# Macaron block (FFN, Mamba scan, FFN) on one core: down products issued in three parts, the next stage's transposes behind the second part

## The chip, the cores and the metric

The kernel runs on one core of a Trainium2 chip. The metric is the device time of one execution in microseconds (us). Before the change the median of three executions is 3233.29 us (3232.2 to 3233.48). A further execution, taken by the profiler, is the source of every row that is shown below.

## What is computed

The input has B, L, H = 4, 1024, 512: 4096 rows of 512 numbers, all fp32. The reference, cut to what matters:

```python
x = x + 0.5 * ffn(layernorm(x))           # stage 1
x = x + mamba(layernorm(x))
x = x + 0.5 * ffn(layernorm(x))           # stage 2

def ffn(x):                               # INTER = 1408
    g = (x @ gate_w.T) * gate_s
    u = (x @ up_w.T) * up_s
    return ((silu(g) * u) @ down_w.T) * down_s

def mamba(x):                             # I = 1024, N = 16, K = 4, R = 128
    h, gate = split(W_in @ x)
    h = silu(causal_conv(h, conv_w) + conv_b)
    ts, Bm, Cm = split(Wx @ h)            # R, N and N numbers, each RMS-normalised
    delta = softplus(Wdt @ ts + dt_bias)
    for t in range(L):                    # in each batch
        s = exp(delta[t] * A) * s + delta[t] * Bm[t] * h[t]
        y[t] = sum_n(s * Cm[t])
    return (Wout @ ((y + D * h) * silu(gate)))
```

## The kernel before

**Chunks and tiles.** The rows are scanned in 16 chunks (`NCS`) of 256 rows, one after another, numbered 0 to 15. The two FFN stages work on tiles of 128 rows. They are not passes of their own: while chunk k is scanned, the FFN of three or four tiles is computed beside it, some of stage 1 for chunks to come, some of stage 2 for chunks already done. The list `BESIDE` fixes how many of each: 3, 3, 4, 4, 3, 4, 4, 3, 4, 4, 3, 4, 4, 3, 3, 3 for chunks 0 to 15. "A three-tile chunk" below means a chunk with three tiles beside it. An FFN has `NF` = 11 blocks of 128 hidden columns; so the down product of one tile is 11 matmuls, each 128x128 by 128x512, summed in one PSUM tile.

**The scan.** In a chunk there are 8 groups of channels (index i) and 4 groups of states (index g), 32 units. In a unit (`unit`) each half does this: ACT makes two exponentials (`da`, L573), POOL a product (`sb`, L578), DVE two scans (L582), a copy of the last state (L587) and a multiplication (`sb`, L592). A half is called a pair in the prediction, since its two scans, its copy and its multiplication go together. Later `add_up` sums a unit's `sb` into `yps` on TensorE, by four matmuls of 128x32 by 128x256 (L604); the sums of an i go out four units at a time. When an i is complete, DVE adds D times u (L611). `head` prepares the step sizes of two further i: the product `dp` of TensorE (L490), which reads `tsT`, then `z` and `dd` on ACT (L498 to L503) and corrections on POOL (L506 to L521). The rest of the preparation is by chunk: the products `hp` for the convolution (L376) and `gp` for the gate (L545), the parameters, and their transposes with the copy into `tsT` (L455).

**The background list.** What lies beside the scan of chunk k is a list of `Work` parts made by `background(k)`. A part has a cost (columns of TensorE work), a share of DVE work (`vector`), a function that emits its instructions, and possibly weight blocks to be loaded. The main loop emits a unit of the scan, then takes parts from the list as long as the part of TensorE's cost done so far is behind the part of DVE's work done so far. A part is never cut: all its instructions come out in one go.

The order in the list is: loads, the first products of the next chunk's preparation, the FFN's `gate_w` and `up_w` products (both L273), between them the gate projections, the output product `op` of the chunk before (L635) and the convolution. The end of the list is what the change touches. There stand the down products (`fo`, L319) and the transposes of the next chunk's FFN tiles (`tp`, L235, made by `flips`). `flips` gives one part that starts the statistics of the first two tiles, and then one part for each tile. That part does a tile's four transposes, defers the copy out of PSUM (L238), and starts the statistics of the tile two further on: `stf` and `mvf` on DVE (L209, L210), `vef`, `rsf`, `nbf` on POOL (L214 to L216), and the normalised tile `xnf` on ACT (L218).

Before, the list ends thus, where `turn` is what `flips` gave and `weave` puts the second list's entries behind the first's:

```python
w, turn = weave(turn[1:2] + f.down(), [NOTHING] + turn[2:])
return parts + w + turn
```

So the order is: transposes of next tile 0, product 0 (all 11 matmuls), transposes of next tile 1, product 1, transposes of next tile 2, and so on.

**What else orders the work.** `defer` holds an emission back until so many further parts with a cost are out; the addition of a down product to its tile (L327) is deferred by one such part, and the store of the tile is handed to SP when two further parts of any kind are out. All loads and stores go through SP's queue, in program order (L101). Weights go through a ring of 14 slots, filled up to 12 blocks ahead. PSUM has a pool of three tiles ("mm") for all products but `da` and `yps`. Instructions that are "pinned" keep their program order on their engine; the others may be moved by the framework's scheduler when the program is built. On the chip each engine runs its list in order.

Of the kernel before, what the change touches and what calls it, by code (L numbers as in the profile page):

```python
# [8 lines left out]
F32 = mybir.dt.float32  # L9
# [4 lines left out]
P = 128  # L14
B, L, H = 4, 1024, 512
# [6 lines left out]
NF = INTER // P  # L22
# [11 lines left out]
HALVES = 14  # L34
LEAD = 12
FRONT = 5
RING = 14

BESIDE = [(3, 0), (3, 0), (2, 2), (2, 2), (1, 2), (2, 2), (2, 2), (2, 1), (2, 2), (2, 2), (2, 1), (2, 2), (2, 2), (1, 2), (0, 3), (0, 3)]
# [3 lines left out]
def macaron_kernel(ctx: ExitStack, tc: tile.TileContext, a: dict, out: bass.AP):  # L43
# [8 lines left out]
    p8 = ctx.enter_context(tc.tile_pool(name="p8", bufs=8))  # L52
    ring = ctx.enter_context(tc.tile_pool(name="ring", bufs=RING))
    dram = ctx.enter_context(tc.tile_pool(name="scratch", bufs=1, space=bass.MemoryType.DRAM))
# [3 lines left out]
    ps_m = ctx.enter_context(tc.tile_pool(name="ps_m", bufs=3, space=PSUM))  # L58
# [27 lines left out]
    down_w = [dram.tile([P, H], F32, name=f"down_w{it}") for it in range(NF)]  # L86
# [56 lines left out]
    def store(out, in_):  # L143
        stores.append([0, out, in_])
# [9 lines left out]
    def defer(parts, emit):  # L154

        deferred.append([parts, emit])
# [7 lines left out]
    def settle():  # L164
        while deferred:
            deferred.pop(0)[1]()
# [18 lines left out]
    NOTHING = Work(0, 0, lambda: None)  # L185

    def then(f, *args):
        return Work(0, 0, lambda: f(*args))

    def cols(t):  # L190
        return t.rearrange("p (k o) -> p k o", k=KH)
# [5 lines left out]
    def silu(t):  # L197

        pin(nc.scalar.activation(t, t, AF.Silu))
        pin(nc.scalar.preload_act_table_set("natural_log_exp_and_others"))  # L200
# [42 lines left out]
    class FFN:  # L243
# [35 lines left out]
        def gate(self):  # L279
            self.done = 0  # L280

            def part(it):
                def emit(w):
                    if it == 0:
                        self.hd = p1.tile([P, NF, 2 * T], F32, tag="hd", name=f"hd{self.name}")
                    gp = self.product("gate_w", it, w[0])
                    nc.scalar.activation(  # L287
                        self.hd[:, it, : self.n], gp, AF.Copy, scale=gate_s[:, it : it + 1]
                    )
                    if it % 4 == 3 or it == NF - 1:  # L290
                        h = self.hd[:, self.done : it + 1, : self.n]
                        silu(h)
                        self.done = it + 1

                return Work(KH * self.n, 0, emit, [("gate_w", it)], settled=it == 0)

            return [part(it) for it in range(NF)]
# [10 lines left out]
            return [part(it) for it in range(NF)]  # L308

        def down(self):  # L310
            wd = []

            def part(t):
                def emit(w=None):
                    wd.extend(w or [])
                    nm = f"{self.name}_{t}"
                    op = ps_m.tile([P, H], F32, tag="mm", name=f"fo{nm}")
                    for it in range(NF):
                        nc.tensor.matmul(  # L319
                            op, lhsT=self.hd[:, it, t * P : (t + 1) * P], rhs=wd[it],  # L320
                            start=(it == 0), stop=(it == NF - 1),
                        )
                    x = self.x[t]
                    stage, r = self.tiles[t]

                    def added():
                        pin(nc.vector.tensor_tensor(x, x, op, ALU.add))  # L327
                        store(x1[r] if stage == 1 else out[r * P : (r + 1) * P, :], x)

                    defer(1, added)  # L330

                return Work(NF * H, H, emit, [("down_w", it) for it in range(NF)] if t == 0 else ())

            r = [part(t) for t in range(len(self.tiles))]
            r[0].until, r[0].settled = r[-1], True
            return r

# [29 lines left out]
    def prep_conv(k):  # L367
        def part(i):
            def emit(w):
                if i == 0:  # L370
                    st[k]["u"] = p2.tile([P, NI, T], F32, tag="u", name=f"u{k}")
                u = st[k]["u"]
                hp = ps_m.tile([P, 512], F32, tag="mm", name=f"hp{k}_{i}")
                w = cols(w[0])
                for kk in range(KH):
                    nc.tensor.matmul(  # L376
                        hp[:, : K - 1 + T], lhsT=w[:, kk, :], rhs=st[k]["xnT"][:, kk, :],
                        start=(kk == 0), stop=(kk == KH - 1),
                    )
                nc.scalar.activation(  # L380
                    u[:, i, :], hp[:, 0:T], AF.Identity,
                    bias=conv_b[:, i : i + 1], scale=conv_w[:, i, 0:1],
                )

                def taps():
                    for q in range(1, K):
                        pin(nc.vector.scalar_tensor_tensor(  # L387
                            u[:, i, :], hp[:, q : q + T], conv_w[:, i, q : q + 1], u[:, i, :],
                            ALU.mult, ALU.add,
                        ))  # L390
                    if i == NI - 1:
                        defer(1, lambda: silu(u))

                defer(1, taps)

            return Work(KH * T, 4 * T, emit, [("W_in", i)], settled=i == 0)

        return [part(i) for i in range(NI)]
# [250 lines left out]
    def weave(xs, by):  # L649

        r = []
        for n, w in enumerate(xs):
            r.append(w)
            r += by[n : n + 1]
        return r, by[len(xs) :]
# [32 lines left out]
    first = [(1, r) for r in range(2 * J, NCS * J)]  # L688
# [17 lines left out]
    def background(k):  # L706

        f = ffn[k]
        prep = k + 1 if k + 1 < NCS else None
        gates, out_of = gate(k), tail(k - 1) if k else []  # L710
        turn = flips(None, prep) if prep is not None else []
        conv = params = []
        if prep is not None:
            conv, params = prep_conv(prep), prep_params(prep)
            ready[k] = params[-1]
        parts = [then(tail_load, k - 1)] if k else []
        if prep is not None:
            parts.append(then(prep_load, k + 1))
        parts += turn[:1]
        p = [NOTHING] * (4 if k else 0) + gates + turn[1:] + out_of + conv  # L720
        tiles = (f.gate() if k else []) + f.up()
        p = [p[n : n + 2] for n in range(0, len(p), 2)]
        p += [[NOTHING]] * 4 + [[w] for w in params]
        turn = flips(ffn[k + 1], None) if k + 1 < NCS else []
        for n, w in enumerate(tiles):
            parts.append(w)
            for q in p[n : n + 1]:
                parts += q
            if n == len(tiles) - NF and k + 1 < NCS:
                parts.append(then(ffn[k + 1].load))  # L730
            if n == len(tiles) - NF and k + 1 == NCS:
                parts.append(then(tail_load, k))
                parts.append(then(end_load))
            if n == len(tiles) - 2:
                parts += turn[:1]
        for q in p[len(tiles):]:
            parts += q
        w, turn = weave(turn[1:2] + f.down(), [NOTHING] + turn[2:])
        return parts + w + turn

    ready = {}


    start = FFN("p", [(1, r) for r in range(2 * J)])
    down, gate_0 = start.down(), ffn[0].gate()
    turn_f, turn_m = flips(ffn[0], None), flips(None, 0)
    front = flips(start, None) + start.gate() + [then(load_resident)] + start.up()
    front += [down[0], down[1], then(prep_load, 0), turn_m[0], down[2]] + turn_m[1:]
    front += [turn_f[0]] + weave(prep_conv(0), [down[3]] + turn_f[1:])[0]
    front += weave(gate_0[:FRONT], prep_params(0))[0]  # L750
    beside_scan = [background(k) for k in range(NCS)]
    end = FFN("e", last)
    turn = flips(end, None)
    back_end = tail(NCS - 1) + turn + end.gate() + end.up() + end.down()
    for w in front + gate_0[FRONT:] + [w for b in beside_scan for w in b] + back_end:
        if w.blocks:
# [8 lines left out]
    settle()  # L765
    between = gate_0[FRONT:]
    chores = head(0, 0)
# [16 lines left out]
    for k in range(NCS):  # L784
        more = k + 1 < NCS
        parts, n, done, vector = list(beside_scan[k]), 0, 0, 0
# [121 lines left out]
```

## Time and profile before

| what | value |
|---|---|
| median of three executions | 3233.29 us (3232.2 to 3233.48) |
| the profiled execution | 3235.77 us |
| its span in the profile | 3234.0 us |
| mean granted clock of TensorE | 0.978 |
| `fo` (L319) on TensorE | 547.6 us, 1232 matmuls of 599 ns |
| `gate_w` and `up_w` (L273) | 566.9 and 564.8 us, 1408 matmuls each |
| `yps` (L604) | 318.6 us, 4096 matmuls; idle before them 79.1 us |
| scans (L582) on DVE | 1057.0 us (x1536) and 321.2 us (x512) |
| products `sb` (L578) on POOL | 1275.0 us, 1024 of 1273 ns |
| weights of `down_w`, by SP | 187 loads of 256 KB, median 2.8 us to landing |

The engines' rows of the page give busy time, share of the span and number of instructions. A group's row gives the source line, engine and operation, the tile that is written and what is read, the shapes and the count; behind the bar stand busy time and the mean of one; then the idle time just before them, and what ended most of it. A row of the waits view names the instruction that waited, behind the arrow the one that released it, then the total in us, how often, and the longest. A timeline row has the start and the duration in us, then engine, line, operation and tiles; "x22" says that so many like it are put together in one row, so that the row's duration covers them all and what lay between, and a bracket gives the idle time before it and what ended it.

### The profile page before, as it was taken

The page shows a single profiled execution, that of the slowest core. Times are in us where ns is not written, and L with a number is a line of the kernel's source. Part 1 is how long each engine was busy: PE and PEld are TensorE (multiplying, and loading weights), DVE is VectorE, ACT ScalarE, POOL GpSimd, SP SyncE. Part 2 cuts the span into 40 slices and gives each one's busy share as a digit, 9 for nine tenths or more (in the row PEclk, how much of TensorE's full clock was granted, in tenths as well). Part 3 has the DMA queues.
Part 4 walks back from the last instruction along what each step waited for, and adds up shares of the span by engine and source line. Part 5 has one row for each costly group of instructions (what it writes and reads, how often), then busy time and mean ns, then how long its engine had stood idle before and what let it go on. Part 6 is the DMA issues. An engine that isn't in the chain of part 4 may idle for free.

```text
span 3234.0 us, 41940 instructions
## 1 busy us (share of the span) xinstructions
PE 3057.9 (95%) x12448; PEld 1648.7 (51%) x12448; DVE 2474.3 (77%) x4981; ACT 1787.0 (55%) x3535; POOL 1937.7 (60%) x1895
## 2 busy tenths in 40 slices
PE   8988898999999999999999999989999998989999
PEld 3554454545555454545545555545555554544434
DVE  1259788888869898887979798787969788788831
ACT  3265554747565664747565564747556474655430
POOL 0066857566766757566765757576665756667510
PEclk9999998999999999999999999999999999999999
DMA  5364655646566555547565656655565654546431
GB/s 171 113 175 113 179 163 154 172 126 189 140 180 185 173 167 162 162 130 207 137 176 162 177 163 171 177 138 170 141 183 160 177 167 136 178 114 197 143 96 44
DMA packets 287427, 506.43 MB, mean 157 GB/s; under 512 B 32097, under 2 KB 50273, under 8 KB 287201
## 3 DMA queue, kind: packets, MB, share of 16 engines
q1 hardware_dynamic: 285616, 503.31, 54.8%
q8 instruction: 100, 1.64, 0.2%
q14 instruction: 127, 1.03, 0.1%
q10 hardware_dynamic: 1584, 0.45, 0.1%
HBM read 442.03 MB, written 61.60 MB: 156 GB/s over the span
## 4 chain that ended last, share of the span: by engine, by line
PE 62%; DVE 20%; ACT 8%; POOL 4%; issue 4%; DMA 1%; SPq 0%; DVEq 0%; ACTq 0%; POOLq 0%
PE fo L319 13%; PE gate_w L273 12%; DVE da L582 12%; PE up_w L273 8%; PE yps L604 5%; PE hp L376 5%; PE gp L545 5%; PE op L635 4%; DVE sb L592 4%; ACT da L573 3%; POOL sb L578 2%; PE dp L490 1%; PE gate_wp L273 1%; PE gate_we L273 1%; DVE u L387 1%
## 5 line engine op out<-in xcount | busy, mean ns | idle before, releaser
L578 POOL TENSOR_TENSOR sb<-rep,bc 128x512 f32<-128x512 f32 x1024 | 1275.0, 1273 | 448.7 <-PE yps L604 381.7
L582 DVE TENSOR_TENSOR_SCAN da<-da,state,sb 128x256 f32<-128x256 f32 x1536 | 1057.0, 739 | 287.3 <-ACT da L573 253.1
L573 ACT ACTIVATE da<-rep,a_w 128x256 f32<-128x256 f32 x2048 | 899.3, 470 | 538.1 <-DVE sb L592 523.6
L592 DVE TENSOR_TENSOR sb<-da,bc 128x512 f32<-128x512 f32 x1024 | 687.7, 680 | 0.9
L273 PE MATMUL gate_w<-fxT,w_gate_w 128*128 128x384 f32 (+1 forms) x1408 | 566.9, 549 | 5.6 <-ACT dd L499 2.3
L273 PE MATMUL up_w<-fxT,w_up_w 128*128 128x384 f32 (+1 forms) x1408 | 564.8, 551 | 0.8 <-issue 0.4
L319 PE MATMUL fo<-w_down_w,hd 128*128 128x512 f32 x1232 | 547.6, 599 | 0.0
L273 PEld LDWEIGHTS up_w<-fxT,w_up_w 128*128 128x128 f32 x1408 | 266.9, 194 | 250.0 <-issue 156.7
L273 PEld LDWEIGHTS gate_w<-fxT,w_gate_w 128*128 128x128 f32 x1408 | 267.6, 193 | 247.7 <-issue 152.4
L604 PE MATMUL yps<-sb,fold 128*32 128x256 f32 x4096 | 318.6, 392 | 79.1 <-DVE sb L592 70.9
L582 DVE TENSOR_TENSOR_SCAN da<-da,sb 128x256 f32<-128x256 f32 x512 | 321.2, 680 | 79.2 <-ACT da L573 65.5
L319 PEld LDWEIGHTS fo<-w_down_w,hd 128*128 128x128 f32 x1232 | 231.5, 192 | 274.0 <-issue 265.0
L521 POOL TENSOR_SCALAR e<-z 128x512 f32<-128x512 f32 x64 | 124.2, 1941 | 278.6 <-ACT z L502 241.8
L604 PEld LDWEIGHTS yps<-sb,fold 128*32 128x32 f32 x4096 | 125.7, 110 | 275.4 <-DVE sb L592 128.3
L376 PE MATMUL hp<-mxT,w_W_in 128*128 128x259 f32 x1024 | 242.6, 388 | 24.3 <-issue 12.9
L545 PE MATMUL gp<-mxT,w_W_in 128*128 128x256 f32 x1024 | 241.4, 385 | 4.1 <-ACT dd L499 2.2
L376 PEld LDWEIGHTS hp<-mxT,w_W_in 128*128 128x128 f32 x1024 | 193.2, 192 | 82.4 <-issue 34.1
L635 PE MATMUL op<-w_Wout,u 128*128 128x512 f32 x512 | 225.0, 595 | 4.6 <-issue 3.6
L545 PEld LDWEIGHTS gp<-mxT,w_W_in 128*128 128x128 f32 x1024 | 193.5, 191 | 61.9 <-issue 17.9
L287 ACT ACTIVATE hd<-gate_w,gate_s 128x384 f32<-128x384 f32 (+1 forms) x176 | 110.6, 629 | 167.5 <-PE gate_w L273 166.6
L387 DVE SCALAR_TENSOR_TENSOR u<-hp,conv_w,u 128x256 f32<-128x256 f32 x384 | 177.6, 474 | 17.4 <-ACT u L380 14.7
L304 DVE SCALAR_TENSOR_TENSOR hd<-up_w,up_s,hd 128x384 f32<-128x384 f32 (+1 forms) x176 | 117.7, 669 | 61.5 <-PE up_w L273 61.4
(112 smaller groups left out, 2657.9 us busy)
## 6 DMA issues: line engine op xcount, KB each, us to landing
rep<-row SPq DMA_DIRECT2D x512, 256.0 KB, 5.1
w_W_in<-in_W_in_dram SPq DMA_DIRECT2D x256, 256.0 KB, 3.5
w_gate_w<-in_gate_w_dram SPq DMA_DIRECT2D x198, 256.0 KB, 3.9
w_up_w<-in_up_w_dram SPq DMA_DIRECT2D x198, 256.0 KB, 3.1
w_down_w<-down_w SPq DMA_DIRECT2D x187, 256.0 KB, 2.8
row<-dd SPq DMA_DIRECT2D x128, 256.0 KB, 3.2
w_Wout<-in_Wout_dram SPq DMA_DIRECT2D x128, 256.0 KB, 3.4
bc<-bcd SPq DMA_DIRECT2D x64, 256.0 KB, 4.7
```

Source lines behind the costliest of these rows:

```text
L273: nc.tensor.matmul(o[:, : self.n], lhsT=w[:, k, :], rhs=self.xT[:, k, : self.n], start=(k == 0), stop=(k == KH - 1),)
L319: nc.tensor.matmul(op, lhsT=self.hd[:, it, t * P : (t + 1) * P], rhs=wd[it], start=(it == 0), stop=(it == NF - 1),)
L376: nc.tensor.matmul(hp[:, : K - 1 + T], lhsT=w[:, kk, :], rhs=st[k]["xnT"][:, kk, :], start=(kk == 0), stop=(kk == KH - 1),)
L387: pin(nc.vector.scalar_tensor_tensor(u[:, i, :], hp[:, q : q + T], conv_w[:, i, q : q + 1], u[:, i, :], ALU.mult, ALU.add,))
L521: lambda: pin(nc.gpsimd.tensor_scalar(e, z, 1.0, 1.0, ALU.add, ALU.subtract)),
L545: nc.tensor.matmul(gp[:, :T], lhsT=w[:, kk, :], rhs=st[k]["xnT"][:, kk, K - 1 :], start=(kk == 0), stop=(kk == KH - 1),)
L573: e = nc.scalar.activation(da[:, j, :], rep[:, h + j, 0, :], AF.Exp, scale=a_w[:, b0 + h + j, g : g + 1])
L578: nc.gpsimd.tensor_tensor(sb, rep[:, hs, 1, :], d["bc"][:, g : g + 1, :].to_broadcast([P, 2, T]), ALU.mult)
L582: nc.vector.tensor_tensor_scan(da[:, j, :], da[:, j, :], sb[:, j, :], 0.0 if first else state[:, b0 + h + j, g : g + 1], ALU.mult, ALU.add,)
L592: nc.vector.tensor_tensor(sb, da, d["bc"][:, NS + g : NS + g + 1, :].to_broadcast([P, 2, T]), ALU.mult)
L604: nc.tensor.matmul(yp[j * Q : (j + 1) * Q, :], lhsT=fold, rhs=pr[j // 2][:, j % 2, :], start=(g == 0), stop=(g == NS - 1),)
L635: nc.tensor.matmul(op, lhsT=st[k]["u"][:, i, j * P : (j + 1) * P], rhs=wo[i], start=(i == 0), stop=(i == NI - 1),)
```

## The change

A constant `DOWN` = 4 is added. `FFN.down` gives three parts for each tile in place of one: 4, 4 and 3 of the 11 matmuls. The PSUM tile is taken when the first part is emitted, and the addition to the tile is deferred when the last is. The cost of a part is its own matmuls; the DVE share is counted on the last alone. In `background` the transposes of the next FFN's tiles no longer stand between whole products: the first stand ahead of all of them, and those of tile n + 1 stand behind the second part of product n. In the front, the part ahead of the first scan, each entry of `down` is replaced by its three parts, and the last tile's three parts are woven with the preparation of chunk 0. The number of matmuls, of transposes, of loads and of stores stays.

```diff
+DOWN = 4
         def down(self):
-            wd = []
-
-            def part(t):
+            wd, ops = [], {}
+            bounds = [*range(0, NF, DOWN), NF]
+
+            def part(t, lo, hi):
                 def emit(w=None):
                     wd.extend(w or [])
                     nm = f"{self.name}_{t}"
-                    op = ps_m.tile([P, H], F32, tag="mm", name=f"fo{nm}")
-                    for it in range(NF):
+                    if lo == 0:
+                        ops[t] = ps_m.tile([P, H], F32, tag="mm", name=f"fo{nm}")
+                    op = ops[t]
+                    for it in range(lo, hi):
                         nc.tensor.matmul(
                             op, lhsT=self.hd[:, it, t * P : (t + 1) * P], rhs=wd[it],
                             start=(it == 0), stop=(it == NF - 1),
                         )
+                    if hi < NF:
+                        return
                     x = self.x[t]
...
                     defer(1, added)
 
-                return Work(NF * H, H, emit, [("down_w", it) for it in range(NF)] if t == 0 else ())
-
-            r = [part(t) for t in range(len(self.tiles))]
+                first = t == 0 and lo == 0
+                return Work(
+                    (hi - lo) * H, H if hi == NF else 0, emit,
+                    [("down_w", it) for it in range(NF)] if first else (),
+                )
+
+            r = [part(t, *b) for t in range(len(self.tiles)) for b in zip(bounds, bounds[1:])]
...
-        w, turn = weave(turn[1:2] + f.down(), [NOTHING] + turn[2:])
-        return parts + w + turn
+        parts += turn[1:2]
+        each = -(-NF // DOWN)
+        for n, w in enumerate(f.down()):
+            parts.append(w)
+            if n % each == 1:
+                parts += turn[2 + n // each : 3 + n // each]
+        return parts + turn[2 + len(f.tiles) :]
...
-    front += [down[0], down[1], then(prep_load, 0), turn_m[0], down[2]] + turn_m[1:]
-    front += [turn_f[0]] + weave(prep_conv(0), [down[3]] + turn_f[1:])[0]
+    each = len(down) // len(start.tiles)
+    front += down[: 2 * each] + [then(prep_load, 0), turn_m[0]] + down[2 * each : 3 * each] + turn_m[1:]
+    front += [turn_f[0]] + weave(prep_conv(0), down[3 * each :] + turn_f[1:])[0]
```

## The prediction

> **What bounds the kernel now.** I read the busy shares first, then the windows around one projection stage of each kind, then who waits for whom, then the timeline of the worst stage. Each answer narrows the next question.
>
> ```profile
> PE 3057.9 (95%) x12448; PEld 1648.7 (51%) x12448; DVE 2474.3 (77%) x4981; ACT 1787.0 (55%) x3535; POOL 1937.7 (60%) x1895
> ```
>
> TensorE (PE) is the bound, and the change removes no matmul. Only its idle time (3234.0 - 3057.9 = 176 us), its slow spells and the waits hidden in its busy rows can be won. I took windows of 60 us; columns as in the page's first part, then PEclk, DMA share, GB/s. In order they hold the down products of chunks 1, 2, 4, 10:
>
> ```profile
> 490.00:550.00 60.00, 48.59 (x192) 21.04 (x191) 47.88 (x99) 27.64 (x61) 43.28 (x41) 0.86 0.55 151
> 686.00:746.00 60.00, 60.00 (x229) 29.03 (x228) 48.97 (x93) 26.93 (x60) 46.86 (x42) 1.00 0.66 183
> ...
> 1046.00:1106.00 60.00, 54.60 (x212) 26.32 (x213) 54.78 (x117) 30.41 (x67) 51.95 (x47) 0.97 0.61 179
> ...
> 2136.00:2196.00 60.00, 48.58 (x193) 21.33 (x193) 48.09 (x98) 27.69 (x61) 43.89 (x42) 0.86 0.59 158
> ```
>
> A chunk with four tiles beside it (2) keeps PE full at clock 1.00. A chunk with three leaves gaps, and 1 and 10 leave 11 us and a clock of 0.86. The waits view says for what, as total, times, longest:
>
> ```profile
> PE yps L604 <- DVE sb L592: 70.9, 37, 5.3
> PE dp L490 <- DVE tsT L455: 32.4, 15, 3.9
> ```
>
> In chunk 1's timeline (start, duration, engine) PE runs dry twice after the second `fo` and once at the end:
>
> ```profile
> 503.32 9.61 PE L319 MATMUL fo<-w_down_w,hd 128*128 128x512 f32 x22
> 512.86 1.07 PE L604 MATMUL yps<-sb,fold 128*32 128x256 f32 x16
> 517.10 1.73 PE L604 MATMUL yps<-sb,fold 128*32 128x256 f32 x8 [3.17 <-DVE sb L592]
> 521.58 1.73 PE L604 MATMUL yps<-sb,fold 128*32 128x256 f32 x8 [2.76 <-DVE sb L592]
> 523.25 1.12 PE L235 MATMUL tpf<-ident,xnf 128*128 128x128 f32 x4
> 524.15 11.30 PE L319 MATMUL fo<-w_down_w,hd 128*128 128x512 f32 x22
> 535.29 1.03 PE L490 MATMUL dp<-tsT,w_dt 128*128 128x256 f32 x4
> ...
> 543.47 1.73 PE L604 MATMUL yps<-sb,fold 128*32 128x256 f32 x8 [5.28 <-DVE sb L592]
> ```
>
> Why is DVE late at 517? Backwards through three in-order lists:
>
> ```profile
> 497.98 0.23 DVE L210 BATCH_NORM_AGGREGATE mvf<-stf 128x2 f32<-128x6 f32 x2
> 498.22 0.22 POOL L214 TENSOR_SCALAR vef<-mvf 128x1 f32<-128x1 f32 x1 [11.95 <-DVE mvf L210]
> 499.49 0.81 ACT L218 ACTIVATE xnf<-xf,nbf,rsf 128x512 f32<-128x512 f32 x1 [5.71 <-POOL nbf L216]
> 501.57 0.76 DVE L582 TENSOR_TENSOR_SCAN da<-da,state,sb 128x256 f32<-128x256 f32 x1 [3.37 <-ACT da L573]
> ```
>
> The aggregate of the next stage's third tile (`mvf`) stands behind sixteen scans on DVE. POOL stands at the `vef` that needs it for 11.95 us, with its scan products queued behind; ACT stands at the `xnf` that needs POOL; DVE then waits for ACT, and 2.22, 0.90 and 0.51 us more for POOL: 7.0 us lost on DVE, shown on PE as the two waits. POOL's wait view gives `vef` 46.3 us in 4 times, in chunks 1, 10, 13, 14. The last wait has another cause: `dp` stands behind 22 `fo` rows, ACT's `z` waits 8.97 us for it, and the exponentials of the last scan pair queue behind `z`.
>
> **The change part by part.** The diff splits each product 4+4+3; what moves because of it is read from the order of the built program (a list of instructions, without times). Matmuls, DMAs and POOL instructions are the same in number.
>
> *Chunks 1, 10, 14: the wait at `vef` goes.* In the new DVE list this `mvf` stands ahead of those scans (in 13 it does not). Chunk 1 by its own durations: DVE passes 498.2 without stopping; a pair costs 3.9 us (four scans 2.67, two multiplies, two copies), so units 0 to 3 of i=6 are ready at 502.1, 506.5, 510.4, 514.9 (with `u` and the add between) against 507.8, 513.1, 517.6, 522.1. PE: `fo` x4 from 492.3 to 495.7; the second half of i=5, now here, waits for the pair that ends at 497.7: **a new wait of 1.4 us**; 4 + 3 + 8 `fo` with a transpose end at 511.7; sums, transpose, 3 + 11 `fo` and `dp` end at 527.3 (535.3 + 1.0 before). Units 2 and 3 of i=7 are ready at dp + 5.8 and dp + 9.7, since ACT's `da` for both now stand behind `z`. A `gate_w` product of 3.44 us is put between the sums, so PE waits 2.4 and 1.7 us and is through sums and product at 537.6. Before, it was through at 543.47 + 1.66 + 12.00/3 = 549.1. That is 11.5 us. Chunk 10 shows the same rows (3.16, 2.76, 5.28): 11.5. Chunk 14 already had product parts between its sums: 8. Together 31; the bare minimum is the two waits, 3 x 6.0 = 18. I take **27**, nearer the walk, which follows every row.
>
> How much of this is clock? After the waits `fo` x22 took 11.30 instead of 9.61 and the next `gate_w` x24 12.00 instead of 10.57: 3.1 us a stage. [...] The measurement decides; 4 of the 31 are therefore left out.
>
> *Chunks 4, 7.* No `vef` wait there, only the end wait (5.10 in chunk 4). The same product between the sums fills 3.4 us; the earlier half of i=5 meets pairs ready at 1050.9 and 1598.6, so PE waits 0.3 and 1.0. Between 0 and -5.5: **-3**. *Chunk 13:* `vef` stays; the pair of unit 2 falls behind `z` (3.9 us) while a product part fills 3.4: **+1**.
>
> *Chunks 2, 5, 8, 11: `tsT`.* The copy stood behind the last scan pair of i=5; in the new list it stands behind the third. `dp` waited 2.45, 2.46, 1.19 and 1.93 us = 8.0. The transposes it needs ended at 678.0 while the copy began at 681.55, so the wait can go whole. Between 0 and -8: **-6**. The second `dp` also moves ahead of 7 `fo` (7 x 0.86 = 6 us); its `z` is needed only in the next chunk, so I count nothing. The sums of i=6 move 6 us earlier: chunk 2 had their last pair at 699.0, PE arrives near 708; 9 us of cover.
>
> *Interleaving costs.* Runs of `yps` rise from 200 to 217. A run of 32 holds PE for 1.86 us (717.30 to 719.16), one of 16 for 1.00: two halves cost 0.14 more. 17 x 0.14 = **+2.4**. [...]
>
> *Queues.* On SP two stores of finished tiles pass ahead of the next weight loads, and so wait for an add on DVE with the loads behind them. In chunk 1 that add ends near 524, where the first load went at 523.8; it lands in 3.9 us and its product starts near 537: 8 us of cover, nothing counted; uncovered it would cost the lateness once a chunk. PSUM: a `fo` tile lives one transpose longer in the pool of three; its add has the same scans ahead: between 0 and +0.6 us (the transpose row) a tile; I take 0, since PE has its next work in another buffer. Front, chunk 0 and chunk 15: small moves, between -3 and +3, taken as 0.
>
> Sum: -27 - 3 + 1 - 6 + 2.4 = **-33 us** of the profiled execution's 3235.77 (span 3234.0 plus 1.8 around it). The median shown, 3233.29, is 2.5 lower, so 3200.
>
> **The rivals.**
> 1. *Given back.* PE merely arrives earlier at the next thing DVE has to deliver. For it: DVE is 77% busy, and the wait for `tsT` recurs in 15 places. Against: four-tile stages run without gaps. If only the 18 us of bare waits stay and 2.4 is paid: 3218.
> 2. *Nothing that can be told.* Reordering lost in noise: POOL's 381.7 us of waits on `yps` are idle time of an engine that does not bound. 3233.
> 3. *Slower.* One mechanism: ACT's `da` of unit 2, i=7, now behind `z` in chunks 1, 10, 13 and 14. It pays only if DVE is early. If something else holds DVE at i=6, so that it ends the second pair of i=7 later than `dp` + 1.5 us, both last pairs come after `dp`: 4 x 3.9 = 15.6, plus 3 x 1.4 for the early sums, plus 2.4, less 6 at `tsT`: +16, 3249. For it: chunk 13 has just that pattern. Against: in 1, 10 and 14 I find no other waiter in front of POOL.
> 4. *More.* Both clock spells go and all the waits I halved: 3180.
>
> **How the numbers follow.** The forecast 3200 gets 0.53 (its own range 3186 to 3214), rival 1 0.12, rival 4 0.05, rival 2 0.10, rival 3 0.20: five places change order at once, and I have walked only chunk 1 row by row. What a measurement here can tell from no change is about 0.2% (6.5 us), so faster is 0.53 + 0.12 + 0.05 = 0.70, same 0.10, slower 0.20. The range leaves out rival 3 alone: from 3176 to 3240, the upper edge of what counts as no change.
>
> **What would show it.** Right: POOL's wait at `vef` falls from four times to one (about 11 us); `yps <- sb` from 70.9 to some 45 us; `dp <- tsT` from 32.4 to some 25; the clock in the stages of 1 and 10 above 0.93; chunk 13 unchanged. Wrong: POOL or ACT in chunk 1 stopped by a new waiter after 486, unit 2 of i=7 later than before, or fresh waits in the four-tile stages, where I count on full cover.

## The result, and the profile after

The median of seven executions is 3242.38 us (3240.6 to 3245.33), against 3232.47 (3231.43 to 3234.57) for the kernel before, measured beside it: a ratio of 1.003, interval 1.0019 to 1.0042. The change makes the kernel 0.3% slower, which is more than the noise. The forecast was 3200, range 3176 to 3240. The profiled execution has a span of 3243.4 us, 9.4 more than before, at a mean clock of 0.981.

The engines' row of the page after:

```profile
PE 3064.6 (94%) x12448; PEld 1647.1 (51%) x12448; DVE 2471.4 (76%) x4981; ACT 1784.7 (55%) x3533; POOL 1935.4 (60%) x1895
```

Nothing here says why: TensorE's busy time rose by 6.7 us with the same instructions, and its idle time by 2.7. By the groups' rows the busy time rose in `up_w` (+5.7), `dp` (+3.6), `hp` (+2.7), `gate_w` (+2.5) and `fo` (+1.8), and fell in `gp` (-3.8) and `yps` (-2.4). TensorE's waits after (who waits, for whom, total, times, longest):

```profile
PE dp L500 <- DVE tsT L465: 40.3, 15, 4.2
PE yps L614 <- DVE sb L602: 36.1, 32, 3.2
PE hp L386 <- issue: 24.4, 12, 5.9
PE gate_w L274 <- ACT fxT L239: 9.9, 4, 2.5
...
PE tpf L236 <- ACT dd L509: 6.6, 4, 1.7
```

The wait that the change was expected to shorten did shrink: `yps <- sb` from 70.9 to 36.1 us. But `dp <- tsT` rose by 7.9, `hp <- issue` by 11.5, and the last two rows were not among the waits of before: 16.5 us. They add up to 35.9, as much as the 34.8 that were won. So the waits merely changed places, and most of the 9.4 us is time in which TensorE works, but slower (6.7 us more for the same 12448 matmuls); the rows below show it behind several of the new waits.

Where each falls is read from windows. I cut each chunk at four events that every version has: **down stage** from the end of the next chunk's transposes `t` to the last `fo`; **gate stage** from there to the first `op`; **convolution stage** from there to the first `sp`. The last two lie in the list of the chunk that follows. For chunk 1 and its follower, before (window, length, busy times, then clock, DMA share, GB/s):

```profile
481.25:535.45 54.20, 44.13 (x156) 19.79 (x156) 46.61 (x98) 23.01 (x49) 36.38 (x40) 0.87 0.46 124
535.45:593.76 58.31, 53.03 (x245) 30.29 (x244) 41.16 (x85) 41.95 (x81) 43.98 (x42) 0.94 0.61 170
593.76:657.41 63.65, 63.65 (x237) 34.34 (x236) 59.96 (x127) 40.67 (x70) 35.64 (x31) 1.00 0.59 170
```

and after:

```profile
477.81:523.31 45.50, 41.12 (x155) 19.23 (x156) 43.04 (x90) 21.97 (x47) 36.51 (x40) 0.92 0.41 103
523.31:581.09 57.78, 52.51 (x244) 28.93 (x244) 41.35 (x86) 39.49 (x76) 44.33 (x42) 1.00 0.73 207
581.09:649.22 68.13, 65.58 (x237) 35.50 (x238) 57.53 (x119) 42.94 (x76) 30.78 (x27) 0.97 0.56 159
```

The down stage is 8.7 us shorter, the gate stage hardly (0.5), and the convolution stage 4.5 longer: PE was full there at a clock of 1.00, and now has gaps (65.58 of 68.13 us busy) and a clock of 0.97. The same cut of all chunks gives this ledger, each entry the stage's length minus that of before. It holds the runs of the next section too. Each row is one profiled execution; its sum differs by up to 6 us from the difference of the medians. "Four-tile" is the sum over the stages of chunks 2, 3, 5, 6, 8, 9, 11, 12; "convolution" is the stage after 1, 4, 7 and 10; "rest" is what remains of the span, mostly chunk 15 and the end.

| span, us against before | sum | 1, 10, 14 down+gate | 4, 7 down+gate | convolution | four-tile | 0 | 13 | rest |
|---|---|---|---|---|---|---|---|---|
| forecast | -33 | -27 | -3 | no term | -6 and +2.4 | 0 | +1 | 0 |
| **after** | +9.4 | -24.7 | +8.3 | +14.5 | +11.5 | -4.1 | -1.8 | +5.7 |
| a_split_only | -21.6 | -18.7 | +1.6 | 0.0 | +1.2 | -4.5 | -5.0 | +3.8 |
| b_three_only | +18.0 | -9.0 | +6.1 | +14.5 | +6.0 | +0.2 | -1.2 | +1.4 |
| c_1_10_14 | +8.7 | -0.8 | -0.5 | +8.4 | +0.9 | +0.1 | -0.1 | +0.7 |
| d_early4 | -34.8 | -35.0 | -11.9 | 0.0 | +15.1 | -4.6 | -1.5 | +3.1 |
| n_last | -2.0 | -18.6 | +8.1 | 0.0 | +8.4 | -3.5 | -1.4 | +5.0 |
| g_move_only | +11.1 | -14.1 | -4.3 | +17.5 | +17.7 | -4.7 | -1.8 | +0.8 |
| p_early4_pin | +47.5 | -1.6 | +9.3 | 0.0 | +22.3 | -5.0 | +3.0 | +19.5 |
| m_early4_three | -26.1 | -19.0 | -12.9 | 0.0 | +6.9 | -0.2 | -1.9 | +1.0 |
| y_not9 | -29.7 | -26.8 | -11.9 | 0.0 | +10.4 | -4.6 | -1.4 | +4.6 |
| w_before_third | +15.1 | -11.6 | +7.4 | 0.0 | +25.2 | -0.3 | -7.8 | +2.2 |
| w_three_third | -6.7 | -17.1 | -3.2 | 0.0 | +21.2 | -0.3 | -8.7 | +1.4 |
| w_all_third | -10.0 | -16.0 | -1.0 | 0.0 | +14.8 | -4.2 | -3.5 | -0.1 |

**The predicted gain is there.** In chunk 1 the aggregate now stands early, and POOL doesn't stop at `vef`, as its timeline row shows by having no bracket. The same holds in 10 and 14:

```profile
495.74 0.22 POOL L215 TENSOR_SCALAR vef<-mvf 128x1 f32<-128x1 f32 x1
```

TensorE's timeline of the end of that stage, to be read against the one of before in the prediction:

```profile
498.89 9.61 PE L323 MATMUL fo<-w_down_w,hd 128*128 128x512 f32 x22
508.43 1.50 PE L614 MATMUL yps<-sb,fold 128*32 128x256 f32 x24
...
512.74 10.57 PE L323 MATMUL fo<-w_down_w,hd 128*128 128x512 f32 x24
523.14 1.03 PE L500 MATMUL dp<-tsT,w_dt 128*128 128x256 f32 x4
525.83 0.66 PE L236 MATMUL tpf<-ident,xnf 128*128 128x128 f32 x4 [1.66 <-ACT dd L509]
526.41 1.07 PE L614 MATMUL yps<-sb,fold 128*32 128x256 f32 x16
529.96 1.98 PE L274 MATMUL gate_w<-fxT,w_gate_w 128*128 128x512 f32 x4 [2.48 <-ACT fxT L239]
531.87 0.64 PE L614 MATMUL yps<-sb,fold 128*32 128x256 f32 x8
```

The waits of 3.17, 2.76 and 5.28 us are gone. What stands in their place is at the end: the transposes of the next FFN's **fourth** tile wait 1.66 us for ACT to empty a PSUM tile, and the `gate_w` product that needs their copy waits 2.48 more. On ACT the copy stands behind `z`, `lg` and exponentials, which are at work until 529.4:

```profile
528.03 1.36 ACT L583 ACTIVATE da<-rep,a_w 128x256 f32<-128x256 f32 x3
529.33 0.58 ACT L239 COPY fxT<-tpf 128x512 f32<-128x512 f32 x1
```

Before, these transposes stood behind `dp` too, and their copy was no earlier: it began at 542.16, 5.4 us after they ended. But the next `gate_w` stood behind the last sums and was not due until 545.12:

```profile
536.16 0.60 PE L235 MATMUL tpf<-ident,xnf 128*128 128x128 f32 x4
536.69 1.50 PE L604 MATMUL yps<-sb,fold 128*32 128x256 f32 x24
...
545.12 12.00 PE L273 MATMUL gate_w<-fxT,w_gate_w 128*128 128x512 f32 x24
```

So the copy's delay was hidden by the wait for the sums. Now `gate_w` goes ahead of the last sums, and the delay shows. The wait before the transposes is new for another reason: in the built program the fourth tile's `tpf` takes over the PSUM tile of `dp`, so ACT's `dd` must have read it; before, it took over that of the second product. All this happens only where a three-tile chunk is followed by a four-tile one (1, 4, 7 and 10, the "4" of the two new rows), since there are three products but four tiles to transpose.

**The unpredicted loss in the convolution stage.** Before, PE and DVE in that stage of the chunk after 1:

```profile
626.77 3.78 PE L376 MATMUL hp<-mxT,w_W_in 128*128 128x259 f32 x16
630.38 3.59 PE L273 MATMUL up_w<-fxT,w_up_w 128*128 128x512 f32 x8
...
631.98 1.51 DVE L387 SCALAR_TENSOR_TENSOR u<-hp,conv_w,u 128x256 f32<-128x256 f32 x3
633.81 3.67 PE L376 MATMUL hp<-mxT,w_W_in 128*128 128x259 f32 x16
```

After:

```profile
614.17 3.77 PE L386 MATMUL hp<-mxT,w_W_in 128*128 128x259 f32 x16
...
617.78 3.60 PE L274 MATMUL up_w<-fxT,w_up_w 128*128 128x512 f32 x8
...
621.28 0.47 DVE L397 SCALAR_TENSOR_TENSOR u<-hp,conv_w,u 128x256 f32<-128x256 f32 x1
...
622.33 0.46 DVE L397 SCALAR_TENSOR_TENSOR u<-hp,conv_w,u 128x256 f32<-128x256 f32 x1
...
623.37 0.46 DVE L397 SCALAR_TENSOR_TENSOR u<-hp,conv_w,u 128x256 f32<-128x256 f32 x1
...
623.93 5.36 PE L386 MATMUL hp<-mxT,w_W_in 128*128 128x259 f32 x16 [2.55 <-issue]
```

Nobody edited this place. A row of `hp` x16 holds two products, and the three taps (`u`) shown read the first of them. They used to come out together and end 2.9 us after the row of `hp` (633.5 against 630.6). Now scans stand between them, and they end 5.9 us after it (623.8 against 617.9). The next `hp` starts 0.1 us after the last tap, and then runs slowly, 5.36 us in place of 3.67: the granted clock was 0.68 from its start to 629.13, and 1.00 for the same row before (633.81 to 637.32).

The profile names no releaser for its wait ("issue"), but the built program does. In both kernels this `hp` takes over the PSUM tile of the `hp` two before it, and must wait for the third tap of that one; the start 0.1 us after the tap agrees. A weight that came late is ruled out: SP issued the last loads for it 30 us earlier (593.4), and the eight loads of `w_W_in` from 566.9 on landed within 5.2 us each. The taps are pinned among themselves; the scans are not, and the scheduler moved them in between. In the built DVE lists of all the runs, the three taps have scans between them in exactly the stages that lost time, and stand together in all the others. Over the four stages 6.2 of the 14.5 us are busy time of TensorE and the rest is idle time.

### The profile page after: what moved, and what is told of

The parts are those of the page before. It is cut to its first block, busy times and chain, and to the rows that moved or that the text cites. A ratio compares the mean times of both kernels' runs of the same rounds, so it can differ in the third digit from the quotient of the medians.

```text
span 3243.4 us, 41949 instructions
## 1 busy us (share of the span) xinstructions
PE 3064.6 (94%) x12448; PEld 1647.1 (51%) x12448; DVE 2471.4 (76%) x4981; ACT 1784.7 (55%) x3533; POOL 1935.4 (60%) x1895
## 4 chain that ended last, share of the span: by engine, by line
PE 57%; DVE 23%; ACT 10%; issue 6%; POOL 3%; DMA 2%; SPq 0%; DVEq 0%; ACTq 0%; POOLq 0%
PE fo L323 14%; DVE da L592 13%; PE gate_w L274 11%; PE hp L386 5%; PE op L645 5%; PE yps L614 4%; DVE sb L602 4%; PE gp L555 4%; PE up_w L274 3%; ACT da L583 3%; DVE hd L305 2%; PE dp L500 1%; PE gate_we L274 1%; PE gate_wp L274 1%; PE foe L323 1%
## 5 line engine op out<-in xcount | busy, mean ns | idle before, releaser
L614 PE MATMUL yps<-sb,fold 128*32 128x256 f32 x4096 | 316.2, 388 | 40.5 <-DVE sb L602 36.1
```

What stands on the lines that cost most here:

```text
L614: nc.tensor.matmul(yp[j * Q : (j + 1) * Q, :], lhsT=fold, rhs=pr[j // 2][:, j % 2, :], start=(g == 0), stop=(g == NS - 1),)
```

## The experiments

Each experiment is a variant of the changed kernel, unless it says "of the kernel before"; all were timed beside the kernel before (medians there 3231.6 to 3232.6). The letters in the expectations: A lays the loss on where the transposes stand, the fourth tile's above all (A1 and A2 are two readings of it: the last sums pushed behind the next product, or the late copy itself); B on the cutting of the products; C on the four-tile chunks; D says that only the cuts in chunks 1, 10 and 14 matter; F that moving the transposes earlier is all of the gain.

**a_split_only**: the cuts stay, each tile's transposes go back behind a whole product.

```diff
-            if n % each == 1:
+            if n % each == each - 1:
```

> Products in three parts as in the changed kernel, but each tile's transposes behind the whole product, as before. Theory A (the loss comes from the late transposes of the fourth tile in chunks 1, 4, 7 and 10, and not from splitting): the waits of gate_w for fxT (2.5 us, 4 times) and of tpf for dd (1.7 us, 4 times) are gone, the new wait of hp (2.5 us in chunks 2 and 5) is gone, and with the wait at vef gone in chunks 1 and 14 the time is under the kernel before: 3210 to 3225 us. Theory B (splitting itself costs, by more changes between products and sums on TensorE): the time stays above the kernel before, 3236 to 3245 us.

3214.46, ratio 0.9947 (0.9935 to 0.996), as A had it. The cut alone gains; B falls. The convolution stages are back to 0.0 and the four-tile chunks cost 1.2. Chunk 10 gains only 1.0 here, since its `vef` wait is back:

```profile
POOL vef L215 <- DVE mvf L211: 22.4, 2, 11.2
```

**b_three_only and c_1_10_14**: cuts and new places only in the three-tile chunks, or only in 1, 10 and 14; elsewhere, and in the front, the list of before.

```diff
+SPLIT = {1, 4, 7, 10, 13, 14}        # c: {1, 10, 14}
-            bounds = [*range(0, NF, DOWN), NF]
+            bounds = [*range(0, NF, DOWN if self.name in SPLIT else NF), NF]
+        if k not in SPLIT:
+            w, turn = weave(turn[1:2] + f.down(), [NOTHING] + turn[2:])
+            return parts + w + turn
```

> The whole change, but only in the chunks with three tiles (1, 4, 7, 10, 13, 14); the chunks with four tiles and the front as before. In its built order mvf of the third tile is late again in chunks 1 and 10 and early in 14. Theory A (late fourth transposes cost in 1, 4, 7, 10 and in the chunk after each): at least as slow as the changed kernel, 3240 to 3255 us, with the four waits of gate_w for fxT and hp waits of about 2.5 us in chunks 2 and 5, though no four-tile product is split there. Theory C (the loss sits in splitting the four-tile chunks): faster than before by the gain of the three-tile chunks, 3205 to 3225 us.

> The change in chunks 1, 10 and 14 alone. The built order keeps mvf of the third tile late in all three, so the wait at vef stays. Theory A: gate_w waits for fxT twice (chunks 1 and 10), hp waits in 2 and 11, none of either in 4, 5, 7, 8; the gain of 1, 10, 14 shrinks to what the end wait gave; 3230 to 3245 us. Theory D (the gain in chunks 1, 10 and 14 comes from putting matmuls between the sums, not from mvf standing earlier): 3205 to 3215 us, as these three stages won 26 us in the changed kernel.

3252.41, ratio 1.0061 (1.0047 to 1.0075), and 3244.71, ratio 1.0038 (1.0026 to 1.0051). C and D fall: without cuts in the four-tile chunks it gets worse. The convolution loss comes exactly with the edited chunks: after 1, 4, 7, 10 in b (14.5), after 1 and 10 alone in c (4.5 and 3.9, and 0.0 after 4 and 7). But chunks 1 and 10, with the same edit as in after, gain at most 1.6 each. Their `vef` waits are back, as the built order had shown, though their own part of the list is the changed one. The waits view of c:

```profile
POOL vef L216 <- DVE mvf L212: 55.7, 6, 12.1
```

So the cut in chunk 1 is not enough to bring its aggregate forward. y_not9 below takes this up. In b the four-tile chunks lose 6.0 us although nothing is edited in them: new `vef` waits stand in 2, 5 and 11 (2.95, 2.94 and 6.24 us), next to edited chunks.

**d_early4**: as after, but the fourth tile's transposes go behind the second product.

```diff
-            if n % each == 1:
+            if n % each == 1 and n // each < len(f.tiles) - 1:
                 parts += turn[2 + n // each : 3 + n // each]
+            if n == (len(f.tiles) - 1) * each - 1:
+                parts += turn[1 + len(f.tiles) : 2 + len(f.tiles)]
```

> The changed kernel with one edit: in chunks 1, 4, 7 and 10 the transposes of the fourth tile stand behind the second product, ahead of the third, in place of behind the third's second part. In the built order they now stand 11 matmuls and a dp ahead of gate_w. Theory A: gate_w's waits for fxT, tpf's for dd and hp's new waits go, the gain in 1, 10 and 14 stays: 3195 to 3215 us. Theory B or C (loss by splitting): 3235 to 3245 us as in the changed kernel.

3201.56, ratio 0.9906 (0.9893 to 0.992): the best of all, and faster than both kernels. The windows of chunk 1 and its follower:

```profile
476.26:523.07 46.81, 42.50 (x167) 20.09 (x170) 46.81 (x98) 28.58 (x63) 38.74 (x42) 0.93 0.41 106
523.07:574.25 51.18, 49.81 (x236) 28.61 (x237) 39.99 (x83) 36.00 (x68) 42.29 (x41) 1.00 0.78 228
574.25:637.89 63.64, 63.64 (x237) 34.34 (x236) 59.40 (x125) 40.38 (x69) 35.17 (x31) 1.00 0.59 170
```

The gate stage is now 7.1 us shorter than before, and the convolution stage is back at 63.64 with PE full. At the end of the stage in TensorE's timeline:

```profile
516.89 6.17 PE L323 MATMUL fo<-w_down_w,hd 128*128 128x512 f32 x14
522.99 1.50 PE L614 MATMUL yps<-sb,fold 128*32 128x256 f32 x24
525.82 1.29 PE L614 MATMUL yps<-sb,fold 128*32 128x256 f32 x8 [1.33 <-DVE sb L602]
527.04 8.42 PE L274 MATMUL gate_w<-fxT,w_gate_w 128*128 128x512 f32 x19
```

`dp` ran at 516.0, so 14 `fo` lie between it and the sums, one short wait is left, and `gate_w` finds its copy ready. In the down stage VectorE is now busy for all of the 46.81 us, so there the bound has moved to it. From after to d the span falls by 44.2 us, all by the place of one tile's transposes in each of four chunks: 20.2 in chunks 4 and 7, 14.5 in the convolution stages, 10.3 in 1, 10 and 14, while the four-tile chunks give back 3.6.

**n_last**: the other direction. The fourth tile's transposes go behind the whole last product, where they were before the change; the rest as after.

```diff
+            if n == len(f.tiles) * each - 1:
+                parts += turn[1 + len(f.tiles) : 2 + len(f.tiles)]
```

(with the first condition of d)

> The changed kernel with the transposes of the fourth tile in chunks 1, 4, 7 and 10 behind the whole third product, and nothing else undone. In the built order these transposes keep their place on TensorE, right behind dp; but the last sums stand ahead of gate_w again, and DVE's list in chunks 2, 5, 8 and 11 has the convolution's steps where they were before. Theory A1 (the order that follows costs: gate_w ahead of the sums, and the convolution's steps in the next chunk): 3215 to 3230 us; gate_w's waits for fxT and hp's 2.5 us are gone, a wait of about 5 us for the last sums is back at four chunk ends. Theory A2 (the late place of the transposes on TensorE itself costs): 3238 to 3245 us.

3229.29, ratio 0.9992 (0.9985 to 0.9998), at the upper end of A1; A2 falls. The transposes stand behind `dp` on TensorE here as in after, so it is not their place there that costs, but the order of what follows. The convolution loss is gone, chunks 4 and 7 still lose 8.1, and the gate stage of chunk 1 is 2.0 longer than before. In this version the last sums come ahead of `gate_w` again, and PE waits for them (`yps <- sb` 51.3 us, against 36.1). So the two ends are about even in the gate stage: PE waits either for the last sums or for the copy. Only with the transposes early, as in d, for neither.

**g_move_only**, of the kernel before: whole products, each tile's transposes one product earlier.

```diff
-        w, turn = weave(turn[1:2] + f.down(), [NOTHING] + turn[2:])
+        w, turn = weave(turn[1:2] + f.down(), turn[2:])
```

> Products whole as before, each next tile's transposes one product earlier. In its built order mvf of the third tile is early in 1 and 10, the sums of i=7 stand behind gate_w in three-tile chunks, and the convolution's steps are early in chunks 2, 5, 8 and 11, as in the changed kernel. Theory A1: the gain at vef in 1 and 10 (16 us) is set off by hp's and tsT's waits in 2, 5, 8, 11: 3225 to 3245 us. Theory F (earlier transposes are all that the good version needs, no split): 3200 to 3212 us.

3246.39, ratio 1.004 (1.0028 to 1.0053), just above A1's range. F falls: moving without cutting loses. It wins 18.4 in chunks 1, 4, 7, 10 and 14, and gives back 17.5 in the convolution stages and 17.7 in the four-tile chunks. So the convolution loss needs no cut and no late transposes: it comes with some orders of emission (after, b, c, g) and not with others (a, d, n_last, p, m, y, and the three w runs).

**p_early4_pin**: d, with the statistics pinned, so that the aggregate can't be moved ahead of scans.

```diff
-        nc.vector.bn_stats(stt, src)
-        nc.vector.bn_aggr(mv, stt)
+        pin(nc.vector.bn_stats(stt, src))
+        pin(nc.vector.bn_aggr(mv, stt))
```

> The early fourth transposes (3202 us), with the statistics on DVE kept in the order of the program, which puts mvf behind all scans of i=5 in chunks 1, 4, 7, 10, 13 and 14. If the forecast's step is right (a late mvf makes POOL wait at vef, and DVE and TensorE behind it), POOL waits at vef in all six, and chunks 1, 4, 7, 10 and 14 lose 6 to 10 us each: 3230 to 3255 us. If the gain of chunks 1, 10 and 14 came from the finer mixture of products and sums: 3198 to 3208 us.

3283.02, ratio 1.0156 (1.0142 to 1.0169): the sign of the first theory, beyond its range, since the pins hold every aggregate, not only the three. The waits view:

```profile
POOL vef L215 <- DVE mvf L211: 107.5, 14, 13.9
```

Against d the down stages lose 12.7 us in chunk 1, 13.4 in 10, 13.6 in 14, and 10.9 and 10.6 in 4 and 7. With `mvf` held behind the scans the wait is there in all six three-tile chunks, 10.6 to 12.6 us each, though the transposes stand as in d. The pins also hold the four-tile chunks' statistics and those of the end, so the 81 us to d are not the price of the three aggregates.

**m_early4_three and y_not9**: d with cuts in the three-tile chunks and the start alone, and d with whole products in chunk 9 alone (edit as in b, and the condition of d).

```diff
+SPLIT = {"p", 1, 4, 7, 10, 13, 14}       # y: {"p", "e", *range(16)} - {9}
```

> The early fourth transposes, with products split in the front and in the chunks of three tiles only. In its built order mvf of the third tile is late in 1 and 10 again. Against the version split everywhere (3202 us): plus 8 us in each of chunks 1 and 10 by the wait at vef, minus what the split costs in four-tile chunks (some 12 us in all by the stage table): 3200 to 3212 us. If the split of four-tile chunks is what helped there: 3215 us or more.

> The early fourth transposes (3202 us), with the products of chunk 9 alone whole again. In the built order chunk 10's down products, transposes and sums stand exactly as in that version on TensorE, but mvf of the third tile falls behind the scans of i=5 on DVE. If the place of mvf decides: the down stage of chunk 10 is 6 to 9 us longer with a wait at vef of about 11 us, chunk 9 at most 2 us shorter, 3204 to 3212 us. If the finer mixture of products and sums in the stage itself decides: chunk 10 unchanged, 3198 to 3203 us.

3209.72, ratio 0.9926 (0.9912 to 0.9939), and 3206.11, ratio 0.9917 (0.9904 to 0.9931), both as their first theories had it. m keeps the four-tile chunks whole, which saves 8.2 us there against d and loses 16.0 in 1, 10 and 14, where the `vef` waits of 1 and 10 are back. y shows why. Chunk 10's own list is that of d; the built orders of PE, POOL and ACT in its down stage are the same, and on DVE only this aggregate stands elsewhere, 38 places later. Yet POOL stops at it, in y:

```profile
2121.48 0.23 DVE L212 BATCH_NORM_AGGREGATE mvf<-stf 128x2 f32<-128x6 f32 x2
2121.72 0.22 POOL L216 TENSOR_SCALAR vef<-mvf 128x1 f32<-128x1 f32 x1 [11.10 <-DVE mvf L212]
```

and in d not:

```profile
2113.72 0.22 POOL L215 TENSOR_SCALAR vef<-mvf 128x1 f32<-128x1 f32 x1
```

Chunk 10's down stage is 7.2 us longer in y (53.9 against 46.7) and its gate stage 0.7. The whole kernel is only 4.6 longer, since the four-tile chunks lose 4.7 less. That is the price of a `vef` wait by itself, measured where nothing else in that stage's order changed: 7.9 us, between the bare 6.0 of the prediction and the walk's 11.5, which had the end wait in it too. It also shows that a chunk's order depends on what its neighbour emits. In d's list, cutting 9 is what helps 10; in a 9 is cut too and 10 waits all the same, so it is no rule.

**w_before_third, w_three_third, w_all_third**: if the late aggregate is the cost, start the third tile's statistics earlier by the list itself: of the kernel before, of m and of d.

```diff
         def start():
             begin(0)
             begin(1)
+            begin(2)
...
-                begin(n + 2)
+                if n:
+                    begin(n + 2)
...
-            if n == len(tiles) - 2:
+            if n == len(tiles) - 3:
                 parts += turn[:1]
```

> The kernel before with whole products; only the statistics of the next stage's third tile start with those of the first two, and all one background part earlier. In its built order mvf of the third tile stands ahead of the scans of i=5 in chunks 1, 10, 13 and 14. If the wait at vef alone holds the gain: no such wait in these chunks, minus 8 us in each, 3195 to 3212 us. If products must be split for it: 3226 to 3240 us.

> Products split in the front and the three-tile chunks, the fourth tile's transposes early, and the statistics of the third tile early too. Against 3210 us without the last edit: minus 8 us in each of chunks 1, 10 and 13, 3180 to 3197 us, if the gains of the two edits lie in different waits and add up; 3203 us or more if they overlap.

> As the last, with the products of four-tile chunks split too. Against 3202 us without early statistics: only chunk 13 still waited at vef, so minus 8 us, 3186 to 3202 us. Above the version that splits in three-tile chunks alone by what the split costs in four-tile chunks (5 to 12 us), if that cost is real.

All three came out far above what was hoped: 3251.57, ratio 1.006 (1.0047 to 1.0072); 3229.23, ratio 0.9989 (0.9981 to 0.9997); 3228.62, ratio 0.9988 (0.9982 to 0.9995). In w_before_third the long wait at `vef` is gone, but another took its place:

```profile
ACT xnf L218 <- POOL nbf L216: 106.0, 40, 7.3
...
POOL vef L214 <- DVE mvf L210: 12.0, 8, 2.3
```

Before, the first of these rows was 79.0 us in 16 times. ACT now stands at three normalisations in a row (7.32, 2.85 and 2.47 us in chunk 1), with the exponentials behind them, and an `fo` waits 3.32 us for ACT's `dd`. Its chunks 1, 10 and 14 gain 11.6 together and 13 gains 7.8, but 4 and 7 lose 7.4 and the four-tile chunks 25.2. In w_three_third and w_all_third the same row grows to 108.4 us (42 times) and 119.0 us (47 times), and `fo` waits 18.3 and 18.0 us in all for `dd`. Starting the statistics early moved the wait from POOL to ACT, and spread it over chunks that had none.

## Why the prediction was wrong

**Right: the `vef` step in chunks 1, 10, 14.** Forecast -27, measured -24.7, and the POOL waits there went as described. Only chunk 13 keeps its wait (11.66), as foreseen. The split between stages was off: the down stages gave -26.3, the gate stages +1.6. The end wait that the walk had down as won was replaced by the waits for ACT, 1.66 and 2.48 in chunks 1 and 10. The step itself, a late aggregate that stops POOL, is shown by y and p. Its cause lay further out than I put it: c and y show that the aggregate's place depends on what the chunk before emits. Where the prediction says that a pair takes 3.9 us, that is a unit, two of the pairs defined ahead of it; the sum is not touched. No run shows the 4 of the 31 us that the sum leaves out for the clock. What the runs show is that both slow spells went in chunks 1 and 10: the last `fo` row, now x24, takes 10.57 us in each, where x22 took 11.30 and 11.08, and the clock of the gate stage is 1.00 in each, where it was 0.94.

**Wrong: no term for the convolution stages, +14.5.** The sum stopped at the next chunk's first products. It followed the DVE list through the down stage and for `tsT`, and took the rest as unmoved; the taps in 2, 5, 8 and 11 had moved, and with PE full before there was no slack. This is the largest error, shown by a, d and n_last, where the stage is back at 0.0 with the cuts in place. Why the scheduler puts scans between the taps in one version and not in another is not settled.

**Wrong: "Chunks 4, 7: -3".** Measured +8.3. The walk had PE fill the end wait with a `gate_w` product and asked nothing of the product's own input. Its copy stood behind ACT's exponentials. The two waits, 4.1 us together in each of 1, 4, 7 and 10, only make up for the end wait that was won, as the gate stage of chunk 4 shows, before and after:

```profile
1079.33:1136.97 57.64, 52.54 (x244) 30.04 (x244) 40.91 (x85) 41.86 (x81) 43.98 (x42) 0.97 0.62 173
1075.10:1136.51 61.41, 56.13 (x244) 29.57 (x244) 40.93 (x86) 39.57 (x76) 44.32 (x42) 0.94 0.63 183
```

PE's idle time is 5.1 us before and 5.3 after. The stage is 3.8 us longer because the same 244 matmuls take 56.1 us in place of 52.5, at a clock of 0.94 in place of 0.97. Of the rest, 4.0 us lie in the down stages of the two chunks and are not traced further. n_last adds that this end cannot be won from there: with the copy's wait gone, PE waits for the sums instead. d, which takes both away, gives -11.9 in the two chunks.

**Wrong: the PSUM term, "I take 0".** The argument was that PE has its next work in another buffer. The fourth tile's transposes take over the tile of `dp` and wait for ACT to read it: 1.66 us four times, 6.6 in all. The queues' term, also 0, held: no wait of TensorE for a load is among its waits after.

**Wrong: "`tsT`, -6".** The wait went from 32.4 to 40.3. The copy does stand a pair earlier in its list, but that is a place, not a time: in chunk 2 it ran 3.4 us after its transposes before (681.55 against 678.15), and 4.1 after them now (674.08 against 669.96). PE had come earlier by more than DVE had, as rival 1 put it. In the whole kernel `dp` and `up_w`, which follow that wait, also take 9.3 us more of busy time. New `vef` waits in 2, 5 and 11 (2.95, 2.95 and 6.25) add to it; I had counted on full cover in the four-tile stages, and their sum is +11.5. It comes with the transposes behind the second part, not with the cuts (a: +1.2), and about half of it with edits in the chunks next door (b: +6.0 with whole products and the old places in the four-tile chunks). How it divides among the waits is not settled. A list with a's places in the four-tile chunks and d's in the others was not tried.

**The interleaving, +2.4**, was not the trouble: in a, with the same cuts, the four-tile chunks cost 1.2 in all. **"Taken as 0"** for chunk 0 and the end held within a few us of each other (-4.1 and +5.7).

**The rivals.** The sign was rival 3's, and its 3249 lies near by chance, for its mechanism did not come about: it placed the loss in chunks 1, 10, 13 and 14, which gained. Of the signs named beforehand, `vef` once was wrong (four times: in 13, and in 2, 5 and 11), `yps <- sb` fell further than said, `tsT` went the wrong way, and "fresh waits in the four-tile stages" was the one that came true. The clock in the stages: 0.92 for both 1 and 10, where I said above 0.93; in the gate stages that follow it rose from 0.94 to 1.00.

## What to carry to other kernels

An edit to a list that a scheduler orders afterwards has to be compared over the whole built program, neighbours included, before any stage is costed as unmoved: here 14.5 us were lost, and in another place 7.2 us hung, on instructions of chunks that nobody touched. When a product is put ahead to fill a wait, follow its own inputs: here `gate_w` reads ACT's copy of the transposes, and that copy queued behind ACT's other work and began 2.8 us after the transposes ended (529.33 against 526.49). And a variant one part away (d against after: 44 us) is worth making before judging the idea.

## What was not expected of the hardware

After a wait of 2.06 or 2.48 us TensorE ran slowly in one chunk and at full clock in another, so the length of the wait doesn't say when. Here are two waits of the same length at the same step of two chunks, in after:

```profile
1416.50 1.13 PE L500 MATMUL dp<-tsT,w_dt 128*128 128x256 f32 x4 [2.06 <-DVE tsT L465]
1417.46 3.60 PE L274 MATMUL up_w<-fxT,w_up_w 128*128 128x512 f32 x8
...
1971.02 1.13 PE L500 MATMUL dp<-tsT,w_dt 128*128 128x256 f32 x4 [2.06 <-DVE tsT L465]
1971.99 5.29 PE L274 MATMUL up_w<-fxT,w_up_w 128*128 128x512 f32 x8
```

The same eight products take 3.60 us and 5.29; the granted clock from the start of `dp` to their end was 1.00 in the first case and 0.73 in the second. The wait of 2.48 us for the copy does the same: behind it the clock was 1.00 in chunk 1 (529.96 to 534.92) and 0.64 in chunk 4 (1081.75 to 1090.35). So in these rows equal waits are followed by different clocks; what decides it, no run here shows. In the second chunk above the slow stretch cost 1.7 us (5.29 against 3.60), nearly another wait.
